# Transposes moved from transfers to TensorE, and attention by seven products in every batch entry

## The chip, the cores and the metric

The kernel runs on one core of one Trainium2 chip. Its time is the device time of one execution in microseconds (us). Three runs of the kernel before gave a median of 1877.63 us (1875.83 to 1879.88). The profile comes from one further execution.

## The reference

One step of a gated block on `src` of shape (4, 2048, 256), float32. With `xn` the layer norm of `src`:

```python
# s: linear attention layer on xn
q, k, v = xn @ Wq + bq, xn @ Wk + bk, xn @ Wv + bv        # 16 heads of 64
Q, K = elu(q) + 1, elu(k) + 1
KV = einsum('bshd,bshm->bhdm', K, v)
Z = 1 / (einsum('bshd,bhd->bsh', Q, K.sum(axis=1)) + 1e-6)
o = einsum('bshd,bhdm,bsh->bshm', Q, KV, Z)
x = layer_norm(xn + o @ Wo + bo, g1, be1)
s = layer_norm(x + gelu(x @ W1 + b1) @ W2 + b2, g2, be2)   # hidden width 1024
# g: gate from a feed-forward net with 4-bit rounding of both operands
quant(t) = per 16 elements of the last axis: scale = max|t| / 6,
           nearest of 0, .5, 1, 1.5, 2, 3, 4, 6 with sign, times scale
h = silu(quant(xn) @ quant(w_gate).T) * (quant(xn) @ quant(w_up).T)  # width 704
g = silu(quant(h) @ quant(w_down).T)
out = src + s * g
```

## The kernel before

**Tiling.** A block is 256 tokens (`T`), held as two tiles of 128 tokens (`TB = 2`). There are 8 blocks per batch entry (`NB`) and 32 in all (`NBLK`). Everything is float32, except for `grid`, the rounded 4-bit values of x and h, which are bfloat16.

**Stages.** First comes a stage over the 8 blocks of the first batch entry that sums keys times inputs (`pk`, `kk`, `pxk`), while weights are loaded and quantized. Then one loop runs over all 32 blocks. In blocks 0 to 23 each iteration also does two of the 16 key sub-blocks of the next batch entry (`subs`): 8 normalize and transpose their input for the first half of the heads, and 8 load both again for the second half. Blocks 24 to 31 belong to the last batch entry and have no keys beside them. From the key sums of an entry, `m_of_half` makes one matrix M (1024 x 256) that stands for attention and `Wo` together; the attention of a block is then `zq` (1024 features by 256 tokens, scaled by Z) times M.

**Order of the work.** TensorE keeps the program's order throughout (`mm` and `tr`, lines 102 to 106, where all its instructions are recorded). DVE and ScalarE keep it up to line 1145; after that a scheduler orders them, held back in places by `tc.issue_after`. DMA is issued almost only by SP, in one queue. PSUM has four tiles under the tag `mm`, shared by nearly all short products and transposes, two under `acc`, two for key sums.

In a block with keys TensorE does, in this order: `pk` of the first sub-block, `pz` (denominators of attention, `sums`), `pxk`, `pg` (gate and up of the next block), `pd` (down), `pk` of the second sub-block, `pa` (attention), `pxk`, part of `py` (second feed-forward product of the block before), `pt_x` (transposes of x1), the rest of `py`, `pq`, `pf` (first feed-forward product). In blocks 24 to 30 it is `pz`, half of `pd`, `pg`, half of `pd`, 4 steps of `py`, `pa`, 16 steps of `py`, `pt_x`, the rest of `py`, `pq`, `pf`.

**Rounded values and their transposes.** `grid_of_h` and `grid_of_x` write `grid` with tokens on partitions; the products need features there. `grid_T` (line 734) has SP issue a transposing transfer into `gridT`, in two pieces per block, late in the block ahead. `spread_scales` (line 717) writes the scales through DRAM into `qT`, also with features on partitions, and `quantized_x` and `quantized_h` (lines 742 and 748) multiply `qT` by `gridT` on DVE.

**Keys' inputs.** `keys_apart` (line 503) has ScalarE part the normalized float32 input into its two 16-bit halves, and SP transposes these by a transfer; `keys_T` (line 524) has ScalarE put them together again as `xnT`. The first two sub-blocks are transposed by TensorE instead.

**Attention.** With seven products of halves (`seven_products`, line 897), the 2 x 2 product of halves costs seven products of 128 columns, each of four steps, instead of eight. It needs four sums of parts of `zq` on DVE before (`attention_sums`, line 924; `s1`, `s3`, `s2`, `s4` of `seven_sums`, line 889), four sums of parts of M on GpSimd once per batch entry (`m_sums`, line 594), and five additions on DVE behind it (`add_seven`, line 907). `in_seven` (line 590) takes it for the first three batch entries. In the last entry `attention` multiplies tile by tile (32 instructions of 256 columns) with one addition behind, and the last block (`attention_by_tiles`, line 952) goes by tiles of tokens, each with its own addition and norm (`attention_norm`, line 966). Every float32 product of 128 rows is two TensorE instructions in the trace.

Of the kernel before, what the change touches and what calls it, by code (L numbers as in the profile page):

```python
# [7 lines left out]

F32 = mybir.dt.float32
BF16 = mybir.dt.bfloat16  # L10
U16 = mybir.dt.uint16
AF = mybir.ActivationFunctionType
ALU = mybir.AluOpType
AX = mybir.AxisListType
# [8 lines left out]
def linear_attention_gated_by_fp4_ffn(  # L23
# [153 lines left out]

    ident = const.tile([P, P], F32, name="ident")
    make_identity(nc, ident)

    warm = mm_tile("warm")
    for _ in range(24):
# [317 lines left out]
            nc.sync.dma_start(xn, xn_d[n])  # L500
            nc.sync.dma_start(xnT, xnT_d[n])

    def keys_apart(b, sub, issue=None):

        f, bi = divmod(sub, NB)
        with tc.issue_after(issue) if issue is not None else nullcontext():
            ones_in(keys[b, sub][0])
        if f > 0:
            return
        n = b * NB + bi  # L510
        half = keys[b, sub][0].bitcast(U16).rearrange("p j (c f h) -> p h c j f", c=ND, h=2)
        apart = work.tile([P, 2, ND, TB, P], U16, tag="e", name=f"apart_{n}", bufs=3)
        with tc.issue_after(issue) if issue is not None else nullcontext():
            for h in range(2):
                scalar.copy(apart[:, h], half[:, h])
        apartT = work.tile([P, 2, ND * T], U16, tag="kk", name=f"apartT_{n}", bufs=3)
        nc.sync.dma_start(
            apartT.rearrange("p h (m t) -> p (h m) t", t=P),
            apart.rearrange("p h c j f -> p (h c j f)"),
            transpose=True,  # L520
        )
        keys[b, sub].append(apartT)

    def keys_T(b, sub, issue=None):

        f, bi = divmod(sub, NB)
        if f > 0:
            return
        n = b * NB + bi
        xn, *apartT = keys[b, sub]  # L530
        xnT = work.tile([P, ND, T], F32, tag="xnT_k", name=f"xnT_k_0_{n}", bufs=3)
        if apartT:
            with tc.issue_after(issue):
                scalar.copy(
                    xnT.bitcast(U16).rearrange("p c (t h) -> p h (c t)", h=2), apartT[0]
                )
        else:
            ones_in(xn)
            scalar.copy(xnT, transposes(xn, f"k_{n}"))
        store_xnT(n, xnT)  # L540
        keys[b, sub] = [xn, xnT]

# [43 lines left out]


    kh, m_sb = {}, {}

    def in_seven(b):  # L590

        return b < B - 1

    def m_sums(b):

# [12 lines left out]
    def m_of_half(b, f, dep=None, ahead=False):  # L608
# [45 lines left out]
        for c2 in range(2):  # L654
# [4 lines left out]
                    start=True, stop=True,  # L659
                )  # L660
            scalar.copy(m[:, 2 * c2 : 2 * c2 + 2, :], pm)
        if f > 0 and in_seven(b):
            m_sums(b)
        yield

# [43 lines left out]
        )  # L709


    gridT = {}

    def chunks_of(h, x):
        return slice(0 if h else NI, NCH if x else NI)

# [14 lines left out]
                by_block[k : k + 1, cs, :].to_broadcast([BLK, wide, T]),  # L731
            )

    def grid_T(n, lo, hi):

        if n not in gridT:
            gridT[n] = work.tile([P, NCH * TB, P], BF16, tag="gridT", name=f"gridT_{n}", bufs=1)
        nc.sync.dma_start(
            gridT[n][:, lo:hi, :], grid[:, lo:hi, :].rearrange("p m f -> p (m f)"), transpose=True
        )  # L740

    def quantized_x(n):

        qx = qT[:, NI:, :]
        t = gridT[n][:, NI * TB :, :].rearrange("p (c j) t -> p c (j t)", j=TB)
        return vector.tensor_tensor(qx, qx, t, ALU.mult)

    def quantized_h(n, j):

        qh = qT[:, :NI, j * P : (j + 1) * P]  # L750
        return vector.tensor_tensor(qh, qh, gridT[n][:, j * NI : (j + 1) * NI, :], ALU.mult)

    def gate_up(n):
        blk[n]["h"] = []
# [175 lines left out]
    def attention(n):  # L930
        x1 = work.tile([P, TB, D], F32, tag="x1", name=f"x1_{n}")
        xn = blk[n].pop("xn")
        b = n // NB
        if in_seven(b):
            pa = [acc_tile(f"pa0_{n}"), mm_tile(f"pa1_{n}")]
            seven_products(
                pa, blk[n].pop("zs"), lambda q: m_sb[b][q], (1, 2, 4, 3, 5, 7, 6), 0, 7 * FOUR
            )
            add_seven(x1, xn, pa)
        else:  # L940
            zq = blk[n].pop("zq")
            pa = acc_tile(f"pa_{n}").rearrange("p (j d) -> p j d", j=TB)
            for j in range(TB):
                for c in range(NH):
                    mm(
                        pa[:, j, :], zq[:, c, j * P : (j + 1) * P],
                        m_sb[b, c // FOUR][:, c % FOUR, :], start=c == 0, stop=c == NH - 1,
                    )
            vector.tensor_tensor(x1, xn, pa, ALU.add)
        blk[n]["x1"] = x1  # L950

    def attention_by_tiles(n):

        x1 = blk[n]["x1"] = work.tile([P, TB, D], F32, tag="x1", name=f"x1_{n}")
        xn, zq = blk[n].pop("xn"), blk[n].pop("zq")
        for j in range(TB):
            pa = (acc_tile, mm_tile)[j](f"pa{j}_{n}")[:, :D]
            for c in range(NH):
                mm(
                    pa, zq[:, c, j * P : (j + 1) * P], m_sb[n // NB, c // FOUR][:, c % FOUR, :],  # L960
                    start=c == 0, stop=c == NH - 1,
                )
            vector.tensor_tensor(x1[:, j, :], xn[:, j, :], pa, ALU.add)
            attention_norm(n, (j,))

    def attention_norm(n, js=range(TB)):
        x1 = blk[n]["x1"]
# [97 lines left out]
    for n in range(NB):  # L1065
        more = n + 1 < NB
        tiles = [(f, j) for f in range(2) for j in range(TB)]
        k, kk = {}, {}

        def product(i):  # L1070
            k[i] = key_product(xnT, *tiles[i], f"0_{n}_{tiles[i][0]}")

        def elu(i):
            f, j = tiles[i]
            kk[i], _ = key_elu(*k[i], f"0_{n}_{f}_{j}")

        def onto_xn(i):
            f, j = tiles[i]
            key_xk(0, f, xn, j, kk[i], n == 0 and j == 0, not more and j == TB - 1)

        product(0)
        if more:
            st = keys_stats(n + 1)
        product(1)
        elu(0)
        product(2)
        dep = kk[0]
        elu(1)
        if more:
            xn_next = keys_norm(n + 1, *st)  # L1090
        elu(2)
        onto_xn(0)
        product(3)
        if 2 * n < 2 * I // P:
            weight = quantize_gu(range(2 * n, min(2 * n + 2, 2 * I // P)))
        else:
            weight = quantize_down(w_down_sb, n - NB + ND)
        step(weight)
        for load in later.get(n, ()):
            load(dep)  # L1100
        onto_xn(1)
        step(ready)
        if n < 2:
            step(constants)
        onto_xn(2)
        elu(3)
        if not more:
            quantized_x(-1)
        if more:
            xnT = keys_xnT(n + 1, xn_next)  # L1110
        step(weight)
        onto_xn(3)
        ready = weight
        if n == 4:
            w_down_sb = load_down()
        if n == 5:
            add_b2(dep)
        if n == 6:
            load_xn(0)
            scales_x(0)  # L1120
            spread_scales(-1, False, True)
            grid_of_x(0)
            grid_T(-1, NI * TB, NCH * TB)
            m_0 = m_of_half(0, 0, dep, ahead=True)
            step(m_0)
        if more:
            xn = xn_next
# [21 lines left out]
        grid_of_h(0, j)  # L1149
    step(m_half)  # L1150
    grid_of_x(1)
    grid_T(0, 0, NCH * TB)

# [14 lines left out]
    for n in range(NBLK):  # L1170
# [49 lines left out]
            down(n, 1)  # L1220
        else:
            for j in range(TB):
                quantized_h(n, j)
                down(n, j)
        with tc.issue_after(blk[n + 1]["late"]) if n < last else nullcontext():
            qz_ins = qz(n)
        if in_seven(b):
            zs_ins = attention_sums(n)
        if not subs:
            ffn_2(n - 1, 4 if n < last else 8)  # L1230
        if n == 0:
# [6 lines left out]
        if n > 0:  # L1238
            with tc.issue_after(kk_ins):
                ffn_sums(n - 1)  # L1240
            if n < last:
                attention(n)
            else:
                attention_by_tiles(n)
        if n < last:
            with tc.issue_after(kk_ins):
                attention_norm(n)
        if n + 2 < NBLK:
            load_xn(n + 2)
        if subs:  # L1250
# [23 lines left out]
            ffn_addend(n, False)  # L1274
        if n == last:
            gate_addend(n)
        for sub in next_subs[: 1 if n == 0 else 2]:
            keys_apart(bn + 1, sub, blk[n]["act"])

        if n > 0 and not subs:  # L1280
            ffn_2(n - 1, 26)
# [3 lines left out]
            ffn_2(n - 1, 28)  # L1285
        if more[0]:
            q_of(n + 1)
        if n == 0:
            keys_apart(bn + 1, next_subs[1], blk[1]["exp"])
        if more[0]:  # L1290
            grid_of_h(n + 1, 0)
            grid_T(n + 1, 0, NI)
            grid_of_h(n + 1, 1, blk[n]["act"])
            if more[1]:
                grid_of_x(n + 2, blk[n]["act"])
                if not subs:
                    attention_addend(n + 2, False)
            grid_T(n + 1, NI, (NCH if more[1] else NI) * TB)
        if n > 0:
            output(n - 1)  # L1300
        if subs and subs[1] % NB == NB - 1:
            step(m_half)
        for sub in next_subs[:1]:
            keys_T(bn + 1, sub, blk[n + 1]["exp"])
        if n + 1 == last:
            ffn_1(n, range(2))
            sums(last)
            ffn_1(n, range(2, NF))
            gpsimd_behind(blk[n]["hT"][:, NF - 1, :])
            gate_addend(n)  # L1310

# [50 lines left out]
```

## Time and profile before

| | |
|---|---|
| median of three runs | 1877.63 us |
| the profiled execution, and its span | 1882.45 us, 1880.7 us |
| TensorE busy, weight loads | 1861.7 us, 1383.0 us |
| DVE, ScalarE, GpSimd busy | 1363.6, 706.7, 386.9 us |
| transposing transfers | 63 of `grid`, 22 of the keys' inputs |
| attention's product per block, by seven and by tiles | 6.25 us, 6.92 us |

Engines are named in the profile as PE (TensorE), PEld (its weight loads, which overlap it), DVE, ACT (ScalarE), POOL (GpSimd) and SP (the queue that issues transfers). A group line has the engine, the operation, output and input, the shapes, the count, then busy us and the mean ns of one, then the idle time ahead of it and what ended it. A timeline line starts with its start and its length, and ends with the idle time ahead of it in square brackets. Instructions of one engine overlap, so busy time divided by the count, or the chain of work, tells what one costs, and the mean of one does not.

### The profile page before, as it was taken

The numbers are of one execution on the slowest core, as the hardware profiler recorded it, in microseconds if no ns is written. First come the engines' busy times: TensorE is split into PE (matmuls) and PEld (weight loads), VectorE is DVE, ScalarE is ACT, GpSimd is POOL, SyncE is SP. The second block draws the span as 40 slices with busy tenths as digits, with TensorE's granted clock in tenths as the row PEclk, the third lists the DMA queues.
The fourth block names the chain that finished last, engine by engine and source line by source line (L and its number), as shares of the span: only waits on it lengthen the run. The fifth ranks groups of instructions, "written<-read, shape, count | busy, mean of one in ns | idle before, by whom it ended". The sixth has DMA issues, their size and how long they took to land.

```text
span 1880.7 us, 25219 instructions
## 1 busy us (share of the span) xinstructions
PE 1861.7 (99%) x9324; PEld 1383.0 (74%) x9324; DVE 1363.6 (73%) x2526; ACT 706.7 (38%) x1191; POOL 386.9 (21%) x371
## 2 busy tenths in 40 slices
PE   9999999999999999999999999999999999999998
PEld 4456677777777777777677787777777788888887
DVE  5676777766677877777667787776676767777775
ACT  2333544333334335443233533353322333333332
POOL 1411322011122212220112221122101122222212
PEclk9999999999999999999999999999999999999999
DMA  5526564434535456635344544564543544444442
GB/s 184 193 73 130 117 124 103 96 101 94 96 64 94 115 98 122 143 66 111 80 89 79 117 100 103 96 139 87 95 86 72 104 75 87 82 90 83 88 84 54
DMA packets 229434, 188.78 MB, mean 100 GB/s; under 512 B 107687, under 2 KB 191155, under 8 KB 229310
## 3 DMA queue, kind: packets, MB, share of 16 engines
q1 hardware_dynamic: 228476, 185.58, 47.4%
q8 instruction: 74, 1.21, 0.3%
q10 hardware_dynamic: 834, 1.58, 0.3%
q14 instruction: 50, 0.41, 0.1%
HBM read 131.96 MB, written 32.59 MB: 87 GB/s over the span
## 4 chain that ended last, share of the span: by engine, by line
PE 78%; DVE 11%; DMA 7%; issue 1%; POOL 1%; SPq 1%; ACT 1%; POOLq 0%; ACTq 0%; DVEq 0%
PE pg L103 13%; PE pf L103 11%; PE pk L103 10%; PE pxk L103 10%; PE pq L103 9%; PE pa L103 8%; PE pd L103 7%; PE py L103 7%; DMA zb<-z_d 3%; PE pz L103 2%; DMA z_d<-z 1%; DVE y L119 1%; DMA xn<-xn_d 1%; DVE x L119 1%; DVE hs L119 1%
## 5 line engine op out<-in xcount | busy, mean ns | idle before, releaser
L430 POOL TENSOR_TENSOR rstd<-rstd,neg_half 128x2 f32<-128x2 f32 (+1 forms) x98 | 77.8, 795 | 1298.0 <-DVE rstd L119 984.9
L103 PE MATMUL pg<-wgu,qT 128*128 128x352 f32 x1024 | 308.5, 459 | 0.1
L103 PEld LDWEIGHTS pg<-wgu,qT 128*128 128x128 f32 x1024 | 194.3, 190 | 113.7 <-issue 11.5
L103 PE MATMUL pk<-wk_sb,xnT_k 128*128 128x512 f32 x512 | 230.4, 592 | 1.2 <-ACT xnT_k L119 1.2
L103 PE MATMUL pq<-xnT,wq_sb 128*128 128x256 f32 x1024 | 227.6, 380 | 1.5 <-DVE zq L119 1.4
L103 PE MATMUL pxk<-kk,xn_k 128*128 128x512 f32 x496 | 227.9, 598 | 1.0 <-DVE kk L119 1.0
L103 PE MATMUL pf<-x1T,w_sb 128*128 128x256 f32 x1024 | 227.2, 380 | 1.1 <-DVE zq L119 0.6
L103 PEld LDWEIGHTS pf<-x1T,w_sb 128*128 128x128 f32 x1024 | 193.8, 190 | 30.4 <-DVE zq L119 4.0
L103 PEld LDWEIGHTS pq<-xnT,wq_sb 128*128 128x128 f32 x1024 | 191.8, 190 | 27.7 <-DVE zq L119 3.1
L119 DVE SCALAR_TENSOR_TENSOR kk<-ek,pk 128x512 f32<-128x512 f32 x128 | 85.6, 685 | 173.2 <-ACT ek L119 173.2
L103 PE MATMUL pd<-wd,qT 128*128 128x256 f32 x768 | 172.9, 380 | 0.0
L103 PEld LDWEIGHTS pk<-wk_sb,xnT_k 128*128 128x128 f32 x512 | 97.0, 190 | 102.6 <-issue 89.0
L119 ACT ACT_TABLE_LOAD x121 | 155.2, 1283 | 40.9 <-PE pk L103 26.0
L119 ACT ACTIVATE x1T<-pt_x,bcol 128x256 f32<-128x256 f32 x64 | 32.7, 561 | 359.3 <-PE pt_x L106 359.3
L103 PEld LDWEIGHTS pd<-wd,qT 128*128 128x128 f32 x768 | 145.3, 190 | 26.4 <-issue 2.5
L103 PEld LDWEIGHTS pxk<-kk,xn_k 128*128 128x128 f32 x496 | 89.4, 190 | 99.1 <-issue 87.3
L119 DVE TENSOR_TENSOR h<-h,pg 128x352 f32<-128x352 f32 x128 | 66.1, 517 | 107.1 <-PE pg L103 104.0
L119 ACT ACTIVATE h<-pg 128x352 f32<-128x352 f32 x128 | 58.9, 460 | 209.8 <-PE pg L103 209.7
L119 ACT ACTIVATE hT<-pf,bcol 128x256 f32<-128x256 f32 x256 | 106.1, 472 | 66.7 <-PE pf L103 66.3
L119 DVE TENSOR_TENSOR zq<-zq,zb 128x1024 f32<-128x1024 f32 x64 | 78.9, 1232 | 68.9 <-DMA zb<-z_d 68.8
L103 PE MATMUL py<-w_sb,hs 128*128 128x128 f32 x992 | 122.0, 275 | 0.0
L119 ACT ACTIVATE e<-pq,neg_one 128x512 f32<-128x512 f32 x128 | 86.2, 685 | 83.7 <-PE pq L103 71.2
(161 smaller groups left out, 2777.8 us busy)
## 6 DMA issues: line engine op xcount, KB each, us to landing
zb<-z_d SPq DMA_DIRECT2D x128, 256.0 KB, 6.2
qT<-scale_d SPq DMA_DIRECT2D x248, 128.0 KB, 6.0
x_k<-in_L_attn_src_dram SPq DMA_DIRECT2D x32, 256.0 KB, 4.1
x<-in_L_attn_src_dram SPq DMA_DIRECT2D x32, 256.0 KB, 2.9
xn_d<-xn_k SPq DMA_DIRECT2D x32, 256.0 KB, 2.5
xn<-xn_d SPq DMA_DIRECT2D x32, 256.0 KB, 2.7
xnT_d<-xnT_k SPq DMA_DIRECT2D x32, 256.0 KB, 2.0
xnT<-xnT_d SPq DMA_DIRECT2D x32, 256.0 KB, 4.3
```

The costliest lines, as they stand in the source:

```text
L103: return tc.keep_in_program_order(nc.tensor.matmul(*args, **kw))
L119: ins = op(*args, **kw)
L430: pool["last"] = nc.gpsimd.tensor_tensor(rstd[:, j0:j1], rstd[:, j0:j1], neg_half[:, j0:j1], ALU.pow).ins
```

## The change

All transposes by transfers go. `grid_T` now makes TensorE transpose the pieces of `grid` as bfloat16 against a bfloat16 identity into a PSUM tile of the tag `mm`, and is called by `quantized_x` and `quantized_h` themselves, whose multiplications read PSUM: 4 transposes for x and 6 for each token tile of h. They stand on TensorE where the multiplications stood in the program: after `pk` and around `pz`, in the last entry also between the halves of `pd`, and for the last block inside the first feed-forward product of the block ahead. `keys_apart` goes; `keys_T` lets TensorE transpose all first-half sub-blocks, the first of each pair between `pq` and `pf`, the second after the transposes of h. `in_seven` and `attention_by_tiles` go: all batch entries use seven products, and the last block has one norm over both tiles.

```diff
+    ident_b = const.tile([P, P], BF16, name="ident_b")
+    nc.gpsimd.tensor_copy(ident_b, ident)
...
-    def keys_apart(b, sub, issue=None):
...
-            for h in range(2):
-                scalar.copy(apart[:, h], half[:, h])
...
-        nc.sync.dma_start(
-            apartT.rearrange("p h (m t) -> p (h m) t", t=P),
-            apart.rearrange("p h c j f -> p (h c j f)"),
-            transpose=True,
-        )
...
+    def keys_T(b, sub, issue=None):
         f, bi = divmod(sub, NB)
+        xn = keys[b, sub][0]
         with tc.issue_after(issue) if issue is not None else nullcontext():
-            ones_in(keys[b, sub][0])
+            ones_in(xn)
         if f > 0:
             return
...
-        if apartT:
-            with tc.issue_after(issue):
-                scalar.copy(
-                    xnT.bitcast(U16).rearrange("p c (t h) -> p h (c t)", h=2), apartT[0]
-                )
-        else:
-            ones_in(xn)
-            scalar.copy(xnT, transposes(xn, f"k_{n}"))
+        scalar.copy(xnT, transposes(xn, f"k_{n}"))
...
-        if f > 0 and in_seven(b):
+        if f > 0:
             m_sums(b)
...
-    def grid_T(n, lo, hi):
-
-        if n not in gridT:
-            gridT[n] = work.tile([P, NCH * TB, P], BF16, tag="gridT", name=f"gridT_{n}", bufs=1)
-        nc.sync.dma_start(
-            gridT[n][:, lo:hi, :], grid[:, lo:hi, :].rearrange("p m f -> p (m f)"), transpose=True
+    def grid_T(name, lo, hi):
+
+        pt = ps.tile([P, 8, P], BF16, tag="mm", name=f"pgrid_{name}")
+        for m in range(lo, hi):
+            tr(pt[:, m - lo, :], grid[:, m, :], ident_b)
+        return pt[:, : hi - lo, :]
+
+    def quantized_x(n):
+
+        qx = qT[:, NI:, :]
+        t = grid_T(f"x_{n}", NI * TB, NCH * TB).rearrange("p (c j) t -> p c (j t)", j=TB)
+        return vector.tensor_tensor(qx, qx, t, ALU.mult)
+
+    def quantized_h(n, j):
+
+        qh = qT[:, :NI, j * P : (j + 1) * P]
+        return vector.tensor_tensor(
+            qh, qh, grid_T(f"h_{n}_{j}", j * NI, (j + 1) * NI), ALU.mult
         )
...
-        if in_seven(b):
-            pa = [acc_tile(f"pa0_{n}"), mm_tile(f"pa1_{n}")]
-            seven_products(
-                pa, blk[n].pop("zs"), lambda q: m_sb[b][q], (1, 2, 4, 3, 5, 7, 6), 0, 7 * FOUR
-            )
-            add_seven(x1, xn, pa)
-        else:
-            zq = blk[n].pop("zq")
-            pa = acc_tile(f"pa_{n}").rearrange("p (j d) -> p j d", j=TB)
...
-            vector.tensor_tensor(x1, xn, pa, ALU.add)
+        pa = [acc_tile(f"pa0_{n}"), mm_tile(f"pa1_{n}")]
+        seven_products(
+            pa, blk[n].pop("zs"), lambda q: m_sb[b][q], (1, 2, 4, 3, 5, 7, 6), 0, 7 * FOUR
+        )
+        add_seven(x1, xn, pa)
...
-            if n < last:
-                attention(n)
-            else:
-                attention_by_tiles(n)
-        if n < last:
-            with tc.issue_after(kk_ins):
-                attention_norm(n)
+            attention(n)
+        with tc.issue_after(kk_ins):
+            attention_norm(n)
...
-            keys_T(bn + 1, sub, blk[n + 1]["exp"])
+            keys_T(bn + 1, sub, blk[n]["act"])
         if n + 1 == last:
             ffn_1(n, range(2))
             sums(last)
-            ffn_1(n, range(2, NF))
+            ffn_1(n, range(2, NF - 2))
+            for j in range(TB):
+                quantized_h(last, j)
+            ffn_1(n, range(NF - 2, NF))
```

## The prediction

> **What bounds the kernel now.** I read the page first, then the chain of work, then the instructions by shape, and last the windows and the timeline of single blocks.
>
> ```profile
> span 1880.7 us, 25219 instructions
> ...
> PE 1861.7 (99%) x9324; PEld 1383.0 (74%) x9324; DVE 1363.6 (73%) x2526; ACT 706.7 (38%) x1191; POOL 386.9 (21%) x371
> ```
>
> TensorE has work in 1861.7 of 1880.7 us: 19.0 us are idle in all. So whatever is added to TensorE is paid, and whatever is taken off the DMA queues, ScalarE or GpSimd pays only through those 19 us. Is a busy TensorE at its rate? Two windows, one block (from one `pz` to the next) with keys beside it and one of the last batch entry, and a third after the last matmul (columns: stretch, length, then busy us of PE, weight loads, DVE, ACT, POOL, granted clock, DMA share, GB/s):
>
> ```profile
> 1418.37:1475.09 56.72, 56.72 (x290) 42.33 (x293) 40.17 (x73) 19.58 (x33) 9.25 (x8) 1.00 0.42 83
> 1708.86:1753.00 44.14, 43.94 (x234) 35.94 (x237) 34.34 (x60) 15.58 (x26) 10.41 (x10) 1.00 0.50 88
> 1875.50:1880.70 5.20, 0.00 (x0) 0.00 (x0) 1.94 (x6) 0.00 (x0) 0.72 (x1) 0.72 0.13 45
> ```
>
> Both kinds of block are full at clock 1.00. DVE has 40.2 of 56.7 us, and 34.3 of 44.1 us: not the bound on average, but not far off in the last eight blocks. The price of a TensorE instruction is read from the chain, since the mean duration of one contains latency that the next one overlaps (start, length, what):
>
> ```profile
> 938.84 0.11 PE pscale L106
> 938.94 1.79 PE py L103 x16
> ```
>
> ```profile
> 1441.08 6.25 PE pa L103 x56
> ...
> 1547.84 6.92 PE pa L103 x32
> ```
>
> A float32 transpose (`pscale`) holds TensorE for 0.11 us, a 128-column float32 matmul instruction for 1.79/16 = 0.112 us (their groups give 283 and 275 ns as the mean of one), and attention's product costs 6.25 us by seven and 6.92 us by tiles.
>
> **The change, part by part.** Counts are per run; "block" is 256 tokens, 32 of them.
>
> *Grid transposes.* Added: 12 for h and 4 for x per block, 32 x 16 = 512 bfloat16 transposes, with their own weight loads. Removed: 63 transposing transfers (7.8 us each to landing, 1.26 us of SP's queue). DVE waited for one of them once, 5.3 us. No bfloat16 transpose is in the trace. From above: the float32 one, 0.110 us. From below by columns:
>
> ```profile
> L106 PEld LDWEIGHTS pt_x<-ident,x x128: 137/141/145, 192.1 to 1859.4; 128*128 128x128 f32 x128
> L106 PE MATMUL pt_x<-ident,x x128: 272/273/332, 192.1 to 1859.5; 128*128 128x128 f32 x128
> ```
>
> Float32 matmuls last 275 ns at 128 columns and 592 at 512 (groups `py`, `pk`): 0.83 ns per column, of which 128 make 106 ns. My estimate from these: at half the bytes half the time, 53 ns, plus the 5 ns that 0.112 has over 0.106: 58 ns. Weight loads (141 ns here, 192 for a matmul's) hide behind that today, at 0.11 us apart. The Trainium skill ("TensorE: Matmul & The Clock Gate", Part 4: PE-mode transpose) says that a bfloat16 transpose takes about 275 ns in a kernel; as a duration the row agrees (273), but charged as such it would make 512 x 0.275 = 141 us, where the chain shows that consecutive transposes start 0.11 us apart. The same page, "Back-to-back issue gap", gives some 81 ns for a bfloat16 pair of load and matmul at 128 columns: 41 us. I take 58 ns (512 x 0.058 = 30 us), because the float32 rows show loads fully covered at 128 columns, and keep 81 and 110 ns for the range.
> In the 24 blocks with keys, plus the first x: 388 x 0.058 = **22.5 us**, all on the path. The other 124 are counted below, where a cycle through DVE sets the time.
> DVE's multiplication reads PSUM instead of SBUF; rows of both kinds at 128x512 take 0.68 us, so nothing.
>
> *Key transposes.* 22 blocks x 4 float32 transposes x 0.110 = **9.7 us**. ScalarE loses two copies of 0.62 and one of 1.33 us per block and gets one of 0.59; it is 38% busy, so nothing. The second of each pair stands on TensorE behind the h transposes and takes the PSUM tile of the x transposes, thus waits for DVE's multiplication by x (kk, kk, x on DVE, ending at about 959.95 in the block of the timeline at 958, when TensorE would arrive at about 959.8): 0.2 us in 12 blocks, **2 us** with what the h tiles wait for `kk`.
>
> *Seven products in the last entry.* TensorE by the chain: 6.25 - 6.92 = -0.67 to -0.8 us (32 x 0.221 = 7.07) per block, 8 blocks. But DVE gets four more sums ahead of the product and five adds in place of one behind it. Block 29 of before shows what is there to cover them:
>
> ```profile
> 1723.44 1.22 DVE L119 TENSOR_TENSOR zq<-zq,zb 128x1024 f32<-128x1024 f32 x1 [1.07 <-DMA zb<-z_d]
> ...
> 1725.44 7.07 PE L103 MATMUL pa<-m,zq 128*128 128x256 f32 x32
> ...
> 1732.35 1.95 PE L103 MATMUL py<-w_sb,hT 128*128 128x128 f32 x16
> ...
> 1732.55 0.69 DVE L119 TENSOR_TENSOR x<-xn,pa 128x512 f32<-128x512 f32 x1 [1.47 <-PE pa L103]
> ...
> 1735.26 0.73 DVE L119 TENSOR_SCALAR x<-x,mv,rstd 128x256 f32<-128x256 f32 x2 [0.82 <-POOL rstd L430]
> ...
> 1735.92 0.68 PE L106 MATMUL pt_x<-ident,x 128*128 128x128 f32 x4
> ```
>
> Behind `pa` stand 32 instructions of `py` (3.57 us) and then `pt_x`, which needs the normalized x1. Now x1 is ready 3.55 us after `pa` ends: exactly covered. In blocks with keys there are 3.44 us of `pxk` and 4.46 us of `py` instead, which is why seven products stalled nothing there.
> The changed kernel's order on DVE, from the end of `zq<-zq,zb` (the zero here): h 0.44; seven sums and hs mixed, 4 x 0.60 + 4 x 0.60; maximum 0.80; scale 0.10; h again 0.80: 6.9. Then x1's five adds (0.60, 0.45, 0.45, 0.36, 0.36 = 2.2) alternate with reciprocal 0.34, grid 0.74, h 0.80, maximum 0.60, scale 0.10; then the first add of s 0.60, statistics 0.70 and 0.13, reciprocal 0.24, s 0.46, rstd 0.10: 14.0. GpSimd's power and back 0.9, the first normalization 0.4: `pt_x` at **15.3**. TensorE: `pa` at 1.6, 6.25, then 3.57: there at 11.4. It stalls 3.9 us, once per block.
> As a cycle: `pz` to the end of qz 14.5 (14.3 now, DMA-bound, plus 0.2 for DVE's multiplication by x ahead of z); 15.3; from `pt_x` to `pf` 9.3; `pf` 6.95; ten grid transposes 0.6; `pz` 1.0: 47.6 against 44.1 us, so 7 x 3.5 = **24.5 us** for blocks 24 to 30, with their transposes and the shorter product in it. What is late next is `pq`, `pf` and so the next block; nothing absorbs it.
> Block 24 has GpSimd's four sums for M (4 x 1.27 us from 1545.0) and an addend ahead of rstd: **1.5 us**.
> *Last block.* Now `pa` is done at 1856.6 and `pt_x` follows at 1859.1 unstalled, because each tile's norm hides behind the other's product. After: the fourth sum stands behind two hs, ready at 1854.7 (stall 1.8); `pa` ends at 1858.4; three adds, statistics, two adds of s, power, norm: `pt_x` at 1863.5. The 12 transposes moved ahead fall into the wait for `zb`. **4.3 us.**
>
> A bfloat16 copy of the identity lies in GpSimd's idle start: nothing. SP's queue loses 85 issues; nobody on TensorE waited for one.
>
> **The sum.** 22.5 + 9.7 + 2 + 24.5 + 1.5 + 4.3 = 64.5 us. The profiled execution took 1882.45 us (span 1880.7 and 1.75 around it), 4.8 above the median of the runs shown; 64.5 on 1877.6 gives **1942**.
>
> One more rule speaks against the change: the same page, "Part 1: The HAM clock gate", says that an idle window of about 3.4 us halves the clock. The third window shows a fall (0.72) after matmuls end; no stall inside is long enough to show one. A 3.9 us stall rarely holds a whole window; if all eight did, half of 3.4 us each is 14 us more. Not in the sum, in the range.
>
> **Rivals.**
> *Only the count matters* (20%): the scheduler's order hides x1 and no stall appears. The last blocks then gain 0.8 and pay 0.9: 22.5 + 9.7 + 2 + about 1 = 35: 1913. For it: DVE has 10 us free per block. Against: these lie elsewhere than in the 11 us between `pa` and `pt_x`.
> *The transposes are slow* (20%): at 81 ns 388 x 0.023 = 9 us more and 1.5 in the last blocks: 1953; at 110 ns 20 + 4 more: 1966; with clock losses 1980.
> *Faster* (4%): the transfers gone, `zb` lands sooner and all idle time goes. At most 19.0 + 6.6 us are won, against 9.7 for the keys: (25.6 - 9.7)/512 = 31 ns is where it decides, well under half the float32 row. Were the grid free: 1862.
> The product by seven in the last entry not paying is inside the forecast: alone it is a loss of some 2.8 us per block.
>
> **How the numbers follow.** Forecast 55% (1926 to 1957 by itself), no stall 20%, slow 20%, faster 4%, equal 1%. From 1912 to 1966 holds about 8 in 10. A change under 0.2% (3.8 us) couldn't be told from none. Faster 0.04, same 0.01, slower 0.95.
>
> **What would show it.** Grid transposes 55 to 60 ns apart; blocks with keys at about 58.5 us (now 56.7), those of the last entry at 47.6; in these an idle of some 4 us before `pt_x`, put down to DVE x; TensorE idle about 45 us instead of 19. Wrong if the last blocks stay at 44 us, or if a block with keys grows by over 3 us.

## The result, and the profile after

The changed kernel takes 1975.3 us (median of four runs, 1974.8 to 1976.1) against 1877.9 us beside it: a ratio of 1.052, 95% interval 1.050 to 1.054. It is slower by 97.4 us. The forecast of 1942 us is 33 us too low and its range, up to 1966, doesn't hold the time.

The head of the page after (span, then busy us of each engine):

```profile
span 1973.8 us, 26634 instructions
...
PE 1909.6 (97%) x10116; PEld 1440.6 (73%) x10116; DVE 1387.6 (70%) x2588; ACT 670.0 (34%) x1147; POOL 381.1 (19%) x375
```

TensorE is busy for 47.9 us more and idle for 45.2 us more (64.2 instead of 19.0 us). Laid out by blocks, from the first `pz` of one to that of the next, the span has grown by 93.1 us:

| stretch | before | after | grown by | predicted |
|---|---|---|---|---|
| `pz` of block 0 to `pz` of block 24 (keys beside) | 1374.6 | 1405.8 | 31.2 | 34.2 |
| `pz` of block 24 to `pz` of block 31 (last entry) | 307.3 | 365.1 | 57.8 | 26.0 |
| from `pz` of block 31 to the end | 45.3 | 49.5 | 4.2 | 4.3 |

So only the middle row is clearly wrong, by 31.8 us, which is almost all of the miss. Windows of one block with keys and one of the last entry after (stretch, length, busy us of PE, weight loads, DVE, ACT, POOL, then granted clock, DMA share, GB/s):

```profile
1441.00:1499.70 58.70, 57.09 (x299) 42.70 (x299) 40.25 (x72) 18.95 (x32) 8.59 (x8) 1.00 0.31 64
...
1720.80:1774.10 53.30, 46.91 (x270) 39.70 (x270) 37.22 (x69) 15.50 (x27) 9.51 (x9) 0.94 0.32 64
```

The second row shows two things at once: 6.4 us in which TensorE stands, and a granted clock of 0.94. The first holds the predicted stall, which came out larger; the second was not in the sum. The timeline of that block, number 27 (start, length, engine, line, output and input, count, and in brackets the idle time ahead and what ended it):

```profile
1723.36 0.33 SPq L762 DMA_DIRECT2D x<-in_L_attn_src_dram  x1
1723.79 0.38 SPq L823 DMA_DIRECT2D z_d<-z  x1
...
1735.76 1.22 DVE L118 TENSOR_TENSOR zq<-zq,zb 128x1024 f32<-128x1024 f32 x1 [1.04 <-DMA zb<-z_d]
...
1741.07 2.05 PE L102 MATMUL pa<-m,zs 128*128 128x128 f32 x16 [1.51 <-DVE zs L118]
...
1751.91 1.26 POOL L646 TENSOR_TENSOR xn<-xn,bo_r 128x512 f32<-128x512 f32 x1
1751.98 1.67 DVE L118 TENSOR_SCALAR x<-x,mv,rstd 128x256 f32<-128x256 f32 x2 [0.60 <-POOL rstd L431]
1753.37 1.23 PE L105 MATMUL pt_x<-ident,x 128*128 128x128 f32 x4 [4.89 <-DVE x L118]
1754.39 2.77 PE L102 MATMUL py<-w_sb,hs 128*128 128x128 f32 x12
```

Read it from the bottom. Twelve `py` take 2.77 us; the same twelve take 1.50 us before:

```profile
1736.43 1.50 PE L103 MATMUL py<-w_sb,hs 128*128 128x128 f32 x12
```

TensorE runs at half speed in the changed kernel. Ahead of it stands the wait for x1, 4.89 us where 3.9 were predicted. Ahead of that, the norm of x1 takes 1.67 us, where it took 0.73 (in the block of before whose lines the prediction shows; it calls it 29, counted from 0 it is 28), and GpSimd's addition to `xn` runs at the very same moment. And 12 us earlier there is a wait that was not predicted at all, 1.51 us ahead of `pa<-m,zs`.

The grid transposes themselves came out as predicted. The chain of work (start, length, what, count) has them 55 and 65 ns apart, while their group gives 220 ns as the mean of one:

```profile
1445.50 0.22 PE pgrid_x L105 x4
...
1446.73 0.78 PE pgrid_h L105 x12
```

```profile
L105 PE MATMUL pgrid_h<-ident_b,grid 128*128 128x128 bf16 x384 | 28.1, 220 | 0.0
L105 PE MATMUL pt_x<-ident,x 128*128 128x128 f32 x128 | 24.2, 309 | 35.4 <-DVE x L118 35.4
```

The second row holds the stall: 35.4 us in all, put down to DVE's x, as the prediction said it would be.

### The profile page after: what moved, and what is told of

The parts are those of the page before. It is cut to its first block, busy times and chain, and to the rows that moved or that the text cites. A ratio compares the mean times of both kernels' runs of the same rounds, so it can differ in the third digit from the quotient of the medians.

```text
span 1973.8 us, 26634 instructions
## 1 busy us (share of the span) xinstructions
PE 1909.6 (97%) x10116; PEld 1440.6 (73%) x10116; DVE 1387.6 (70%) x2588; ACT 670.0 (34%) x1147; POOL 381.1 (19%) x375
## 4 chain that ended last, share of the span: by engine, by line
PE 79%; issue 9%; DVE 5%; DMA 4%; POOL 2%; ACT 1%; SPq 0%; DVEq 0%; ACTq 0%; POOLq 0%
PE pg L102 11%; PE pxk L102 11%; PE pf L102 10%; PE pk L102 10%; PE pq L102 10%; PE py L102 8%; PE pa L102 7%; PE pd L102 6%; DMA zb<-z_d 1%; PE pt_x L105 1%; DVE qT L118 1%; PE pt_k L105 1%; DVE x L118 1%; PE pm L102 1%; POOL rstd L431 1%
## 5 line engine op out<-in xcount | busy, mean ns | idle before, releaser
L102 PE MATMUL py<-w_sb,hs 128*128 128x128 f32 x992 | 132.2, 289 | 0.0
L102 PEld LDWEIGHTS py<-w_sb,hs 128*128 128x128 f32 x992 | 126.7, 206 | 0.0
```

The costliest lines, as they stand in the source:

```text
L102: return tc.keep_in_program_order(nc.tensor.matmul(*args, **kw))
```

## The experiments

Two theories at the start. A: seven products in the last entry make x1 late, TensorE waits for it, and the clock falls after the wait. B: the transposes by TensorE, which also reach into the last entry, delay the denominators there, and the product by seven matters little.

### The parts of the change, one by one

`e1_tiles_last` is the changed kernel with attention of the last entry as before (tiles, and tiles of tokens in the last block):

```diff
+    def in_seven(b):
+        return b < B - 1
...
-        zs_ins = attention_sums(n)
+        if in_seven(b):
+            zs_ins = attention_sums(n)
...
-            attention(n)
+            if n < last:
+                attention(n)
+            else:
+                attention_by_tiles(n)
```

> The changed kernel with the last batch entry's attention by tiles of 256 columns and its last block by tiles of tokens, as before; all transposes stay on TensorE. Theory A (the seven products in the last entry make x1 late, TensorE stalls about 4.9 us ahead of pt_x and its clock is halved for some us): about 55 us of the 97 go, 1918 to 1925 us, blocks 24 to 30 at 45 us, no 0.5 clock inside. Theory B (the grid's transposes delay z and zb in the last blocks, whatever product follows): the last blocks stay above 49 us, 1950 or more.

`e2_seven_only` is the reverse: the kernel before, with seven products in the last entry and nothing else (`in_seven` always true, one norm in the last block).

> The kernel before with seven products in the last entry too, and nothing else: transposes stay with transfers. Theory A: blocks 24 to 30 at 49 to 51 us instead of 44.1, with a stall of 4 us or more ahead of pt_x and the clock falling: 1915 to 1925 us. Theory B: 1872 to 1880 us.

`e3_grid_only` is the kernel before with the grid transposed by TensorE, `e4_keys_only` the kernel before with the keys' inputs transposed by TensorE (`grid_T` and `keys_T` as in the diff above).

> The kernel before with the transposes of the grid alone on TensorE. Theory A: 512 transposes at 58 ns, 30 us, on the path in all blocks: 1905 to 1912 us. Theory B: 1925 or more, since the last blocks stall.

> The kernel before with the transposes of the keys' inputs alone on TensorE. Both theories: 88 float32 transposes at 0.11 us, 9.7 us, and little waiting: 1886 to 1890 us.

| kernel | us | ratio to before (1877.9), 95% | against before |
|---|---|---|---|
| grid alone (e3) | 1906.3 | 1.015 (1.013 to 1.017) | +28.4 |
| keys alone (e4) | 1885.4 | 1.004 (1.002 to 1.005) | +7.5 |
| grid and keys, last entry by tiles (e1) | 1918.3 | 1.021 (1.020 to 1.023) | +40.4 |
| seven products alone (e2) | 1933.9 | 1.030 (1.028 to 1.031) | +56.0 |

B falls: without any transpose of the other kind, the seven products lose 56 us. A holds, though e2 was expected to lose less (1915 to 1925 us). The three parts alone add up to 91.9 of the 97.4 us. In e1 a block of the last entry is full again at clock 1.00:

```profile
1696.30:1741.80 45.50, 45.24 (x250) 36.97 (x246) 33.83 (x61) 15.58 (x27) 9.87 (x11) 1.00 0.34 75
```

### Is it the clock?

`e5_filled` puts work that changes nothing into the wait:

```diff
         if n > 0:
             ffn_2(n - 1, 20)
+            for _ in range(0 if subs or n == last else 5):
+                seven_products(blk[n - 1]["py"], blk[n - 1]["ffn"], w2, (1, 2, 4, 3, 5, 7, 6), 16, 20)
```

> The changed kernel, with five repeats of products 16 to 20 of the FFN before (20 matmuls of 128 columns, about 5.6 us of work by the 0.28 us of a pa, that only write again what they have written) put in TensorE's order just ahead of the transposes of x1 in blocks 24 to 30; nothing is left out. The wait ahead of pt_x was 4.9 us in each of these blocks and the clock was at half for 3.4 or 6.8 us after it. Theory A (the idle wait lowers the clock): the granted clock stays at 1.00 in the last entry, pt_x to pf falls from 12.2 to about 9.5 us, py x12 from 2.77 to 1.5 us; the work put in lasts about 0.7 us longer than the wait, so a block is some 2 us shorter: 51.5 us instead of 53.4, the kernel at 1957 to 1964 us. Rival (what follows the wait is slow for another reason: the activations or the banks are late): the blocks stay at 53 us or more and the kernel at 1973 us or above.

It takes 1967.3 us (1.046, 1.044 to 1.048). First a window after the wait in the changed kernel, then the one that answers to it in e5:

```profile
1750.00:1770.00 20.00, 16.63 (x74) 14.99 (x75) 13.38 (x28) 9.47 (x15) 5.70 (x5) 0.83 0.44 69
```

```profile
1740.00:1768.00 28.00, 27.57 (x197) 24.76 (x195) 20.76 (x45) 11.70 (x20) 5.85 (x7) 1.00 0.37 69
```

The clock stays at 1.00 in blocks 24 to 30, and block 27 takes 50.9 us instead of 53.4, though 4.5 us of useless products lie in it (40 instructions of 0.112 us, not the 5.6 us of the expectation). So the slow `py`, `pq` and `pf` behind the wait are the clock's doing, and the clock falls because TensorE stands. The kernel as a whole is above the expected range: blocks 24 to 30 give 12.0 us back, but the stretch after the last `pz`, in which nothing was filled, takes 52.2 us instead of 49.5. In e5 the clock falls to half for 3.41 us in the middle of that stretch, and in the changed kernel only after its last product; there is also a wait of 1.05 us ahead of `pa<-m,zq` that the changed kernel doesn't have.

### Is it GpSimd beside the norm?

`e7_addend_later` makes GpSimd's addition to `xn` wait until the norm and the two operations on x1 are done:

```diff
                 if not subs:
-                    attention_addend(n + 2, False)
+                    gpsimd_behind(blk[n]["x1"][:, TB - 1, :])
+                    attention_addend(n + 2)
```

> The changed kernel, with GpSimd's addition to xn in the last entry placed behind the norm of x1 and the addend of the FFN, so that GpSimd and VectorE don't work on 512 columns each at the same moment; nothing is left out. Theory (GpSimd's operation beside the norm is what made it 1.67 us instead of 0.73): the norm takes 0.7 us, the wait ahead of pt_x falls from 4.9 to about 3.9 us, and a block is 1 us shorter, or 2 to 4 where the clock then falls for less long: 1960 to 1969 us. Rival (the norm is slow by where its operands lie or by its own wait): the norm stays at 1.6 us and the kernel at 1973 to 1977 us.

1968.8 us (1.048, 1.046 to 1.049), in the expected range. Its timeline:

```profile
1752.84 0.73 DVE L118 TENSOR_SCALAR x<-x,mv,rstd 128x256 f32<-128x256 f32 x2 [0.60 <-POOL rstd L431]
...
1753.31 0.87 PE L105 MATMUL pt_x<-ident,x 128*128 128x128 f32 x4 [3.96 <-DVE x L118]
```

The norm is back at 0.73 us and the wait at 3.96 us, which is the 3.9 of the prediction. Why did the two never meet before? In the kernel before, GpSimd's addition had to wait for DVE's `y`, which reads the same `xn` and came after the norm:

```profile
1739.93 1.85 POOL L676 TENSOR_TENSOR xn<-xn,bo_r 128x512 f32<-128x512 f32 x1 [0.62 <-DVE y L119]
```

In the changed kernel x1 is so late that `y` passes it on DVE, and that sets GpSimd free just when the norm begins.

### Is it where TensorE waits, or VectorE's chain?

`e6_later_x1T` gives TensorE half of the next queries to do in the wait; GpSimd's two operations on x1 (`ffn_addend`) move along:

```diff
-        x1_T(n)
-        if not subs:
-            ffn_addend(n, False)
+        if subs or not more[0]:
+            x1_T(n)
+            if not subs:
+                ffn_addend(n, False)
...
-        if more[0]:
+        if more[0] and subs:
             q_of(n + 1)
+        elif more[0]:
+            q_of(n + 1, range(NH // 2))
+            x1_T(n)
+            ffn_addend(n, False)
+            q_of(n + 1, range(NH // 2, NH))
```

> The changed kernel, in blocks 24 to 30 with the transposes of x1 placed between the two halves of the next block's queries instead of ahead of them, so that 6.8 us of TensorE's work lie in the wait; nothing is left out. Theory A (the only loss is TensorE standing and its clock after it): no wait over 3 us is left, the clock stays at 1.00, blocks of 45 to 46.5 us against 53.4, and the kernel at 1929 to 1936 us. Rival (VectorE's own chain from pz to the next pz is what takes the time, wherever TensorE waits): the wait comes back ahead of pf, pz or pa, blocks of about 48 us or more, and the kernel at 1945 us or above.

1953.1 us (1.039, 1.038 to 1.041): better by 22 us, but the rival's time, not A's. The wait for x1 is gone and the clock is 1.00 in its block 27; the block still takes 48.2 us, and TensorE works in 44.3 of them:

```profile
1715.10:1763.30 48.20, 44.31 (x273) 37.12 (x270) 37.10 (x69) 15.34 (x27) 9.59 (x11) 1.00 0.35 70
```

```profile
1736.04 2.05 PE L102 MATMUL pa<-m,zs 128*128 128x128 f32 x16 [1.99 <-DVE zs L118]
...
1746.87 1.26 POOL L646 TENSOR_TENSOR xn<-xn,bo_r 128x512 f32<-128x512 f32 x1
1746.94 1.67 DVE L118 TENSOR_SCALAR x<-x,mv,rstd 128x256 f32<-128x256 f32 x2 [0.59 <-POOL rstd L431]
...
1750.66 1.26 POOL L786 TENSOR_TENSOR x<-x,shift_r 128x512 f32<-128x512 f32 x1
...
1750.90 1.30 DVE L118 SCALAR_TENSOR_TENSOR s<-s,mv,g 128x256 f32<-128x256 f32 x1
...
1752.86 1.99 PE L102 MATMUL pq<-xnT,wq_sb 128*128 128x256 f32 x8 [1.90 <-DVE zq L118]
```

The wait has come back in two places. At `pq` it is again a meeting of GpSimd and DVE, now two of them: the norm, and the subtraction of the mean of s (1.30 us; its group before has 0.49 as the mean). Block 24 stays at 57.7 us, with a wait of 5.00 us at `pq` and half clock behind it.

`e8_best` makes the same move in the kernel before, with seven products in blocks 24 to 30 and the last block by tiles.

> The kernel before, with three edits: the seven products of halves in blocks 24 to 30, the transposes of x1 of these blocks between the halves of the next block's queries, and the last block by tiles as before; the transposes by transfers stay. Nothing is left out. Theory A (the seven products save 4.5 us of TensorE's work a block, and cost only by the wait that they bring ahead of pt_x): blocks of about 42.5 to 43.5 us instead of 44.1, and the kernel at 1866 to 1875 us. Rival (VectorE's chain, longer by the sums and additions, sets the block wherever TensorE's work is put): blocks of 46 to 48 us, and the kernel at 1890 to 1905 us.

1906.4 us (1.014, 1.012 to 1.015), the rival's time again. Its block 27 has 43.2 us of work where before has 43.9, so the seven products do save TensorE 0.76 us (not the 4.5 us that the expectation names), and it has 1.90 us of waiting at `pq`, so that is lost. Most of the 25.0 us that blocks 24 to 30 lose lies at their two ends: block 24 grows by 10.7 us and block 30 by 6.5, with waits of 4.30 and 3.10 us at `pq` and half clock in both. The runs e12 and e13 below leave these two blocks out.

### GpSimd's operations out of the way

`e10_gpsimd_later` takes e6 and moves GpSimd's two operations on x1 and the one on `xn` behind the last queries (the lines that take them out of their old places are left out here):

```diff
         if n > 0:
             output(n - 1)
+        if not subs and n < last:
+            gpsimd_behind(blk[n + 1]["zq"][:, NH - 1, :])
+            ffn_addend(n)
+            if more[1]:
+                attention_addend(n + 2)
```

> The kernel with the transposes of x1 between the halves of the queries (blocks 24 to 30), and GpSimd's three additions and multiplications on 512 columns of these blocks (the two for x1, the one for xn) behind VectorE's last part of the queries, instead of beside the two norms; nothing is left out. Theory C (VectorE's chain is late because its operations wait for GpSimd's at the same moment: the norm of x1 1.67 instead of 0.73 us, the subtraction of the mean of s 1.30 instead of 0.47): both take 0.5 to 0.8 us, the 1.9 us wait ahead of pq goes, blocks of 45.5 to 46.5 us against 47.6 with the moved transposes alone, and the kernel at 1936 to 1945 us. Rival (VectorE's chain is too long by its own operations): the waits stay, blocks of 47 us or more, the kernel at 1950 us or above.

1940.5 us (1.032, 1.031 to 1.034), as theory C expected: 12.7 us less by moving three operations on an engine that is busy for a fifth of the time. In blocks 26 to 29 `pq` no longer waits; block 27 takes 46.4 us, with 44.4 us of work at clock 1.00:

```profile
1739.30 0.73 DVE L118 TENSOR_SCALAR x<-x,mv,rstd 128x256 f32<-128x256 f32 x2 [0.59 <-POOL rstd L431]
...
1742.33 0.47 DVE L118 SCALAR_TENSOR_TENSOR s<-s,mv,g 128x256 f32<-128x256 f32 x1
...
1750.39 2.90 DVE L118 SCALAR_TENSOR_TENSOR grid<-m_x,y 128x256 bf16<-128x256 bf16 x2
...
1751.56 1.45 POOL L646 TENSOR_TENSOR xn<-xn,bo_r 128x512 f32<-128x512 f32 x1
```

But GpSimd now meets the rounding of x: 2.90 us for two operations that take 0.75 in e6, with two of GpSimd's beside them. Here it costs TensorE 0.6 us ahead of `pgrid_x`.

`e11_and_x_three` adds a third buffer for the tile `x` (`bufs=3`), to let SP load it without waiting for GpSimd.

> The kernel with the moved transposes of x1 and GpSimd's later additions, and with a third buffer for the tile x, so that SP's load of x needn't wait for GpSimd's addition that reads the one before, and z_d behind it in SP's queue is issued at once; nothing is left out. Theory (the load of x holds z_d up by 0.4 to 0.55 us): the reciprocal of z to z_d falls below 0.6 us, the wait ahead of pa<-m,zs falls by about 0.5 us in each block, and the kernel is 3 to 5 us below the one without the third buffer. Rival (z waits for its transfers, however early they are issued): the same time within 2 us.

1940.3 us (1.032, 1.030 to 1.034), no difference. It settles nothing: SP's load of x still starts the moment GpSimd's `o<-o,x` ends, so the buffer was not what held it. What `z_d` loses behind that load stays unmeasured.

`e12_five_blocks` is the kernel before with seven products in blocks 25 to 29 only, with both moves of e10. The sums for M come after the product of block 24, and M is put together again after that of block 29.

> The kernel before, its transposes by transfers kept, with seven products of halves in blocks 25 to 29 alone, with the transposes of x1 moved between the halves of the queries and GpSimd's additions behind them in these blocks; the sums for M are made after the product of block 24, and M is put together again after that of block 29. Nothing is left out. Theory (without waits the seven products save TensorE 0.76 us a block): blocks of 43.2 to 44 us against 44.1, the kernel at 1873 to 1879 us, no loss and a gain that can hardly be told from none. Rival (VectorE's chain alone is too long for the block): blocks of 45 us or more, the kernel at 1883 to 1892 us.

1896.6 us (1.009, 1.008 to 1.010), worse than either theory said. The first of its five blocks takes 43.3 us, less than the 44.1 of before; the next four take 47.1 to 49.0. The timeline between blocks 27 and 28:

```profile
1708.60 1.33 POOL L821 TENSOR_TENSOR x<-x,shift_r 128x512 f32<-128x512 f32 x1
1708.73 2.90 DVE L119 SCALAR_TENSOR_TENSOR grid<-m_x,y 128x256 bf16<-128x256 bf16 x2
...
1711.66 1.35 SPq L742 DMA_TRANSPOSE gridT<-grid  x1
...
1715.08 0.77 DVE L119 TENSOR_TENSOR qT<-qT,gridT 128x512 f32<-128x512 f32 x1 [2.58 <-DMA gridT<-grid]
```

The slowed rounding of x here stands ahead of a transposing transfer, and behind that stand `pg`, z and the next product. So the same meeting that cost e10 0.6 us lies on the path here, and these four blocks take 3.8 to 5.7 us more than the first, with the waits and the half clock behind it. That is read from the timeline; e13 tests it.

`e13_addends_next` moves the three operations once more, behind those on g and o in the next block, where DVE mostly waits for `pg` (one line: `keys_beside` is also true in these blocks).

> The same five blocks by seven products in the kernel before, with the moved transposes of x1, but GpSimd's two operations on x1 and the one on xn placed behind those on g and o in the next block, while TensorE is at pg and VectorE waits for it. Nothing is left out. Theory C (with GpSimd clear of the norms and of the rounding of x, the first of these five blocks, 43.3 us, is what all of them take): no wait over 0.5 us in blocks 25 to 29, clock 1.00, blocks of 43.3 to 43.8 us against 44.1, and the kernel 2 to 5 us below the one before: 1874 to 1878 us against 1879.5. Rival (it meets another operation of VectorE there, or the sums themselves make VectorE late): blocks of 45 us or more, and the kernel at 1883 us or above.

1878.1 us against 1879.5 us beside it: 0.9990, interval 0.9984 to 0.9997. Blocks 25 to 29 take 43.3, 44.0, 44.2, 44.4 and 44.2 us.

```profile
1662.00:1706.30 44.30, 43.30 (x256) 36.18 (x255) 35.60 (x68) 15.41 (x27) 10.47 (x10) 1.00 0.49 89
```

```profile
1681.31 2.05 PE L103 MATMUL pa<-m,zs 128*128 128x128 f32 x16 [0.88 <-DVE zs L119]
...
1702.15 0.75 DVE L119 SCALAR_TENSOR_TENSOR grid<-m_x,y 128x256 bf16<-128x256 bf16 x2
```

With everything moved out of the way (the norm is at 0.73 us too), the seven products in these blocks cost nothing: 220.1 us for the five, against 221.9 before. The gain of the kernel is 0.1%, between 0.03 and 0.16%: clear of none by this interval, and no more than that, because the 0.7 us that TensorE saves in a block (43.2 us of work against 43.9) is used up by the wait at `pa<-m,zs`, 0.88 us in this one. Theory C had no wait over 0.5 us; four of the five blocks have one of 0.59 to 1.04 us there.

## Why the prediction was wrong

**Grid transposes: right.** 58 ns each was the estimate, 55 to 65 the measured spacing, and e3 gives 28.4 us for 512, or 55 ns (22.5 us, or 44 ns, between the two profiled executions, of which the one before lies 4.8 us above its median). A price taken from what precedes and follows on the chain was the right kind; the mean of one (220 ns in the bfloat16 row; the 273 in the prediction is a float32 row) would have made it four times as much. The rival of slow transposes falls with it, and that of a faster kernel too.

**Keys: right, slightly high.** 9.7 us plus part of 2 us of small waits were predicted; e4 has 7.5.

**Seven products in the last entry: right mechanism, wrong size.** The rival that no stall appears falls with e2. The stall lies where it was put, ahead of `pt_x`, and for the reason given. The failed step is "As a cycle": 47.6 us for a block, where block 27 takes 53.4. In the prediction's own terms, forecast and then measured in block 27: from `pz` to the end of `qz` 14.5 and 16.2; from there to `pt_x` 15.3 and 16.4; from `pt_x` to `pf` 9.3 and 12.2; `pf` 6.95 and 7.07; transposes and `pz` 1.6 and 1.6. Seen from TensorE, the 47.6 were 43.7 us of work and 3.9 of waiting. Of the other 5.8 us:

| term in block 27 | predicted | measured | from |
|---|---|---|---|
| clock at half after the wait | 0 | 2.7 | work 47.0, against 44.3 in e6 at clock 1.00 |
| wait ahead of `pa<-m,zs` | 0 | 1.5 | its timeline |
| wait ahead of `pt_x` | 3.9 | 4.9 | 3.96 in e7 without GpSimd beside the norm |
| TensorE's work at full clock | 43.7 | 44.3 | e6 |

The 0.6 of the last row is a misreading: from `pt_x` to `pf` this block of before already took 9.9 us, not 9.3. Over blocks 24 to 30 the same terms are 14.9 us for the clock, 9.6 against 1.5 (block 24) for waits ahead of `pa`, 31.3 against 27.3 for those ahead of `pt_x`, and seven times 0.6: together 31 of the 31.8 us.

*The clock.* The prediction had the rule (the Trainium skill, "TensorE: Matmul & The Clock Gate", Part 1: The HAM clock gate: half speed after an idle window of about 3.4 us) and set it aside, because a stall of 3.9 us would "rarely" hold a whole window. That step failed: here the window need not be idle as a whole. The granted clock in the trace falls to 0.5 eight times in blocks 24 to 30, at least once in each, and behind five of the eight falls lie windows in which TensorE was busy for 7 to 50% (the last section has the rule that the traces show). In all it is at 0.5 for 41.0 us there, and TensorE works in 35.8 of them. In e10, where it is at 0.5 for only 3.41 us in these blocks, TensorE does the same work in 14.9 us less (309.3 against 324.3 us): almost half of the miss in the middle row. The 14 us that the prediction held back for it were near the size; they stood in the range and not in the sum.

*GpSimd beside DVE.* The prediction took 0.4 us for the first normalization from a block where GpSimd was idle at that moment. It followed the order on DVE, but didn't ask what that order sets free on GpSimd. The Trainium skill has the rule ("SBUF — State Buffer", Who interferes with whom: GpSimd and some VectorE operations share one pair of ports, and one of the two waits for the other's whole instruction). The runs agree with it: 0.73 and 1.67 us, 0.47 and 1.30, 0.75 and 2.90, each time with GpSimd operations of 1.26 to 1.45 us beside it, and back again when these are moved (e7, e10, e13).

*The wait ahead of `pa`.* In the changed kernel it is 0.6 to 1.5 us in blocks 25 to 30. In e2, without the grid transposes, it is 0.2 us at most in five of these blocks, but 1.75 in block 26. The denominators reach `zq` later: in block 27 the end of `zq<-zq,zb` is 16.2 us behind `pz`, where the prediction had 14.5. It took 14.3 from before, where blocks 25 to 29 have 14.0 to 17.6, and added 0.2 us for DVE's multiplication by x ahead of z. SP issues `z_d` behind its load of x, which waits for GpSimd (first two lines of the timeline of block 27). That is 0.55 us behind the reciprocal of z in block 27, where before has 0.03. How the rest is shared between that queue and the transfer itself was not settled (e11).

*Block 24.* Here the prediction added 1.5 us for GpSimd's four sums of M, 5.0 us with the cycle; the block grows by 9.8 (47.1 to 56.9). The sums take 1.59 to 1.76 us each, not 1.27, while two of DVE's sums beside them take 1.75 instead of 0.68; TensorE waits 2.27 us for the last of them ahead of `pa<-mt,zq`, and the clock falls behind that wait as well as behind the one at `pt_x`. What moving these sums would bring was not tested.

**Last block: right, with some luck.** 4.3 us predicted, 4.2 measured, and the stall at the fourth sum is 1.7 us where 1.8 was forecast. But in e5, e6, e7 and e10 the same two waits (1.7 us, then 2.2 ahead of `pt_x`) are followed by 3.41 us of half clock, and this stretch takes 51.2 to 52.2 us instead of 49.5.

**The base.** The sum was laid on the median of 1877.6 us, while the trace that it was worked out from is 4.8 us above it. The trace after grew by 93.1 us and the medians by 97.4, so 4.3 of the 33 us are this.

## What to carry to other kernels

Where a reordering brings a wait of 4 us or more into TensorE's stream, charge the wait and then a few us of half clock behind it; and ask what the new order on VectorE lets GpSimd start, since an operation that meets GpSimd can take more than twice its time (0.73 and 1.67 us here). Saved matmul columns are worth only what is left after the sums that they need: here 0.76 us a block at best, and it took three moved operations on an engine that is 20% busy to get even that close. If a wait can't be avoided, moving independent matmuls into it pays at once (22 us in e6).

## What was not expected of the hardware

The length of a wait alone didn't tell whether the clock falls. After every wait of 3.8 to 5.2 us ahead of `pt_x` it fell, in the changed kernel and in e7, for 3.41 or 6.83 us. After a wait of 3.01 us there, in block 30, it fell in the changed kernel and not in e7. After the five waits of 1.90 us at `pq` in e6 it never fell; after the four waits of 1.99 us at `pa<-m,zs` in e12 it fell three times, for 3.41 us each.

What tells is how a wait lies on a fixed grid. In each of the 14 traces all changes of the granted clock are whole multiples of 3.41 us apart. Cut every trace into windows of this grid, from 20 us on up to the last product, and take the share of each in which TensorE is busy. At full clock, half clock followed all 36 windows that were busy for less than 42%, 7 of the 24 between 42 and 51%, and none of those above. At half clock, it stayed behind all 13 windows of up to 83%, and full clock came back behind all 43 of 87% or more. Two of the waits of 1.99 us in e12, in blocks 26 and 29 (length, busy us of PE, weight loads and DVE, then clock):

```profile
1635.22:1638.63 3.41, 1.42 (x13) 1.23 (x12) 3.41 (x6) 0.00 (x0) 0.00 (x0) 1.00 0.00 0
1638.63:1642.05 3.42, 3.42 (x19) 3.42 (x18) 3.42 (x8) 0.00 (x0) 0.00 (x0) 0.50 0.00 0
...
1778.60:1782.01 3.41, 1.78 (x16) 1.59 (x15) 3.41 (x7) 0.00 (x0) 0.00 (x0) 1.00 0.00 0
```

The first wait lies in one window, leaves it busy for 42%, and the next window has half clock. The second lies across the end of its window, leaves it busy for 52%, and the clock stays. From these shares follows an estimate: 2 us of waiting within one window of 3.41 us bring half clock, so a wait of 4 us always does, wherever it lies, and one of 1.7 to 4 us does or doesn't by where it lies. Where the grid lies differs from one execution to the next: the falls stand at another offset in each trace.

A bfloat16 transpose with its own weight load costs TensorE 55 to 65 ns, half of a float32 one, and in a block of 46 us sixteen of them came to 1.0 us (44.3 us of work in e6 against 43.3 in e13, which has the transfers).
